# A pre-activation block on one core: where the last centroid rows of two tables are subtracted, and from where the spare rows come

## The chip, the core and the metric

The kernel runs on one core of one Trainium2 chip. The metric is the device time of one execution in microseconds (us). A core has five engines that run side by side, each with its own instruction queue worked off in order: PE (TensorE, matrix products), DVE (VectorE), ACT (ScalarE), POOL (GpSimd) and SP (SyncE, which here only issues DMAs). An engine that waits in front of one instruction holds up all that is queued behind it.

## The reference, cut to what matters

The input x has 32 images of 1024 channels and 14 x 14 positions. Two residual layers are computed. The first one consists of three table layers ("amm"), each followed by a batch norm; the second one is a linear attention and is not touched by the change.

```python
def _amm(patches, centroids, lut, inv_temp):
    v = patches.reshape(B, ncb, sub, H*W).transpose(0, 3, 1, 2)
    scores = 2.0*einsum('blcs,cks->blck', v, centroids) - sum(centroids*centroids, -1)
    attn = softmax(scores*inv_temp, axis=-1)          # over the K = 16 centroids of a codebook
    return einsum('blck,cko->blo', attn, lut)         # lut: codebooks x 16 x outputs

out = _amm(x, c1_centroids, c1_lut, c1_invt)          # layer 1: 256 codebooks of 4 channels, 256 outputs
out = relu(_bn(out, bn1_g, bn1_b))
out = _amm(_extract3x3(out), c2_centroids, c2_lut, c2_invt)   # layer 2: 256 codebooks of 9, 256 outputs
out = relu(_bn(out, bn2_g, bn2_b))
out = _amm(out, c3_centroids, c3_lut, c3_invt)        # layer 3: 64 codebooks of 4, 1024 outputs
return relu(_bn(out, bn3_g, bn3_b) + identity)
```

Layers 1 and 2 have tables of 4096 rows (256 codebooks with 16 rows each) by 256 outputs. Since the 16 weights of a codebook add up to one, a codebook's last row can be subtracted from its other fifteen: that moves the output by a constant per channel, which the batch norm takes out again. The last row's place is then free.

## The kernel before, in words

**Units.** A pass of layers 1 and 2 goes over 16 pairs of images (392 positions) and, in each pair, over 8 units b = 0..7, so over 128 units u = 8 p + b. A unit has four tiles of 128 rows: eight codebooks by 16 centroids. Its steps are: the scores on PE (L897 in layer 1; L1015 and L1024 in layer 2), the exponentials on ACT (L595, written to t), a transpose on DVE (L607), in layer 1 a halving of the sums on POOL (L610), the sum, the reciprocal and a transpose back on DVE (L625, L627, L633), the product with the reciprocals on POOL (L637), and the product with the unit's table on PE (L702, "lut(u)"), which collects all eight units of a pair in two PSUM tiles `po`. ACT's L638 adds up the sums for a check of overflow and waits for the reciprocals. A unit's scores are worked four units (layer 1) or three (layer 2) ahead of its table product; six tiles t rotate.

**Spare rows.** Of four units that follow one another, the first one's first tile (j = 0) is not multiplied as a tile of its own. Its 120 rows other than last ones go into the free last places (rows 15, 31, ...) of the other fifteen tiles, eight rows each. For the weights, POOL writes the tile to `spare` (L635), and small DMAs on SP spread it (L684, `t<-spare`, three or four for each unit). For the tables the same rows have to be in the same places. The eight tables `weights[b]` (512 KB each, named `lut` in the profile) hold a layer's whole table and are loaded again for layer 2.

**Tables before.** For each b, SP issues `own` (L424: the unit's rows), `others` (L427: the spare rows, into every sixteenth partition), and `last_rows`: three or four DMAs that spread each codebook's last row over 16 partitions in a scratch tile d (L439), with a fifth for the spare rows' own last row (L442). One subtraction `v - d` on POOL or DVE (L445, `less`) then ends the table. The scratch lies in the free end of `out1` in layer 1 and in x tiles in layer 2. Layer 1's eight subtractions are put among the first units (`side(i)` runs the pieces that `at(i, ...)` has filed under i, ahead of `lut(i)`); layer 2's eight all stand on POOL after the last unit of layer 1.

**From layer 1 to layer 2.** When lut(127) is done, DVE and POOL work out the norm's scale (L312 to L329, L242), ACT writes the normed images of pair 0 to `pad` (L932, `store_pair`), SP stores them to DRAM (L943, `h1d<-pad`), and SP loads the shifted copies that layer 2's scores need (L963, `patch<-h1d`). Meanwhile DVE builds layer 2's biases and score matrices (L375 on, PE's L390 between), and PE runs dummy products (`warm`, L590). Order on each engine in these layers is the order in which the program issues; nothing reorders it.

**PSUM.** `ps_po` has three rotating buffers; before, only the table products use them. Four more hold scores.

Of the kernel before, what the change touches and what calls it, by code (L numbers as in the profile page):

```python
# [10 lines left out]
F32 = mybir.dt.float32  # L11
AF = mybir.ActivationFunctionType
ALU = mybir.AluOpType
AX = mybir.AxisListType
# [3 lines left out]
P = 128  # L18
C = 1024
CT = C // P  # L20
HW = 196
N2 = 2 * HW
# [3 lines left out]
KC = 16  # L26
W = 256
# [123 lines left out]
def conv_preact_kernel(ctx: ExitStack, tc: tile.TileContext, a: dict, out: bass.AP):  # L151
    nc = tc.nc
    x = a["x"]
    B = x.shape[0]
    NP = B // 2
    NTOK = B * HW
# [37 lines left out]
    ident = const("ident", [P, P], eng=ENG.Activation)  # L194
    mask2 = const("mask2", [72, 8], a["mask2"][1:73])
    bn = {}
    for i, n in ((1, 2), (2, 2), (3, CT)):
        bn[i] = (const(f"bn{i}_g", [P, n]), const(f"bn{i}_b", [P, n]))
    ones = cp.tile([P, P], F32, tag="ones", name="ones")
    nc.vector.memset(ones, 1.0)  # L200
    mhalf = cp.tile([P, 16], F32, tag="mhalf", name="mhalf")
    nc.vector.memset(mhalf, -0.5)
# [209 lines left out]

    def unit_rows(layer, b):
        return lut1_tiles[b] if layer == 1 else lut2_tiles[b // 4, b % 4]

    def packed_lut(layer, b):

        rows, spare = unit_rows(layer, b), unit_rows(layer, b - b % 4)[0]
        j0 = 0 if b % 4 else 1
        k0 = 4 * (b % 4) + j0 - 1  # L420
        v = weights[b].rearrange("p (s w) -> p s w", s=4)

        def own():
            nc.sync.dma_start(v[:, j0:], rows[j0:].rearrange("j c k w -> (c k) j w"))  # L424

        def others():
            nc.sync.dma_start(v[15::16, j0:], spare[:, k0 : k0 + 4 - j0])  # L427

        return v, own, others

    def last_rows(d, layer, b):


        rows, spare = unit_rows(layer, b), unit_rows(layer, b - b % 4)[0]
        j0 = 0 if b % 4 else 1
        v = weights[b].rearrange("p (s w) -> p s w", s=4)
        d = d.rearrange("p (s w) -> p s w", s=4)
        for j in range(j0, 4):
            nc.sync.dma_start(d[:, j], rows[j][:, 15:].to_broadcast([8, KC, W]))  # L439

        def others():
            nc.sync.dma_start(d[15::16, j0:], spare[:, 15:].to_broadcast([8, 4 - j0, W]))  # L442

        def less(engine=nc.gpsimd):
            engine.tensor_tensor(v[:, j0:], v[:, j0:], d[:, j0:], ALU.subtract)  # L445

        return others, less

    sums = cp.tile([P, 3], F32, tag="sums", name="sums")
    sc3 = cp.tile([P, CT], F32, tag="sc3", name="sc3")  # L450
# [75 lines left out]
    def layers(exact, early=None):  # L526
# [59 lines left out]
        def warm(n, rhs):  # L586

            t = scores(rhs.shape[1])
            for _ in range(n):
                nc.tensor.matmul(t, ident, rhs, start=True, stop=True)  # L590
# [70 lines left out]
        def unit_tiles(n):  # L661
# [6 lines left out]
            return ts  # L668


        spares = [
            (dram if exact else big).tile([P, N2], F32, tag=f"spare{exact}{k}", name=f"spare{k}")
            for k in range(2)
# [71 lines left out]
        with ExitStack() as s:  # L745
# [11 lines left out]
            def at(i, piece):  # L757
                todo.setdefault(max(i, -AHEAD - 1), []).append(piece)
# [46 lines left out]
                    at(8 * p + c - AHEAD - 1 - (p == 0), normalise(p, c))  # L805
            at(24, edges)
            at(40, masks2)
            for b in range(8):
                if b > 5:
                    at(b - 6, lambda b=b: load_rows(b))  # L810
                if b > 3:
                    at(b - 5, lambda b=b: others(b))
                engine = nc.vector if b in (3, 5, 7) else nc.gpsimd
                at(b - 3 if b > 1 else -99, lambda b=b, engine=engine: lasts[b][1](engine))

            def later():
                if not exact:
# [3 lines left out]
                load_raw2()  # L821

            at(16, later)

            lasts2, room = {}, {}

            def load_last2(b, k, n):
                def piece():
                    if n == 0:
                        room[k] = xp.tile([P, CT, N2], F32, tag="x", name=f"x_{NP + k}")  # L830
                    d = room[k].rearrange("p c n -> p (c n)")[:, n * C : (n + 1) * C]
                    lasts2[b] = last_rows(d, 2, b)

                return piece

            end = 8 * NP
            for k, bs in ((0, (3, 4, 5)), (1, (0, 1, 2)), (2, (6, 7))):
                for n, b in enumerate(bs):
                    i = end - 8 * (2 - k) + n + (0 if k < 2 else -3)
                    at(i, load_last2(b, k, n))  # L840
                    at(i + 1, lambda b=b: lasts2[b][0]())
            for b in range(7):
                at(end - 7 + b, luts2[b][1])
                if b < 6:
                    at(end - 6 + b, luts2[b][2])

            luts = [packed_lut(1, b) for b in range(8)]

            lasts = []

            def load_rows(b):
                luts[b][1]()
                d = out1[:, b // 4, NTOK - (b % 4 + 1) * C :][:, :C]
                lasts.append(last_rows(d, 1, b))

            def others(b):
                luts[b][2]()
                lasts[b][0]()

            xts[0] = load_x(xp, 0)  # L860
            for b in range(6):
                load_rows(b)
                if b == 1:
                    xts[1] = load_x(xp, 1)
                if b % 2 == 0 and b:
                    others(b - 2)
                    others(b - 1)
            if not exact:
                masks()
            bias1, biases = score_biases(ps_tr, once, st, 1, raw[1], P, CT, mask8, 4)  # L870
            w1 = score_matrices(once, 1, "", raw[1], mask8)
            gn = [
                gn_pieces(sm, ps_tr, xts[p], gn_a[:, :, v], gn_b[:, :, v])
                for p, v in ((0, slice(0, 2)), (1, slice(2, 4)))
            ]
            warm(14, xts[0][:, 0, :HW])
            for f in gn[0][:-1]:
                f()
            if not exact:
                kmasks()  # L880
            ts = unit_tiles(AHEAD + 2)
            biases()
            warm(14, xts[0][:, 1, :HW])
            gn[0][-1]()
            for p in range(2, NP):
                at(8 * p - 17, load(p))
# [25 lines left out]
                halve=not exact,  # L912
            )
            luts2[7][1]()
            luts2[6][2]()
            luts2[7][2]()
            for b in range(8):
                lasts2[b][1]()
            add_up(0, 8 * NP)


        with ExitStack() as s:
# [7 lines left out]
            def store_pair(p, h):  # L930
                t = pads[2 * (p % 2) + h]
                nc.scalar.activation(  # L932
                    t.rearrange("p (i r c) -> p i r c", r=15, c=15)[:, :, :14, :14],
                    out1[:, h, p * N2 : (p + 1) * N2].rearrange(
                        "p (i r c) -> p i r c", r=14, c=14
                    ),
                    AF.Relu,
                    bias=bi1[:, h : h + 1],
                    scale=sc1[:, h : h + 1],
                )  # L940
                for x in range(3):
                    c0 = LEAD + 2 * p * IMG + 1 - DX[x]
                    nc.sync.dma_start(  # L943
                        h1d[16 * h : 16 * h + 16, 8 * x : 8 * x + 8, c0 : c0 + 2 * IMG], t
                    )
# [10 lines left out]
            def load_patches(n, b0=0, m=4, js=range(4)):  # L956
                p, h = divmod(n, 2)
                for j in js:
                    for r0, dy, k in TAPS:
# [7 lines left out]
                            ),  # L967
                        )

            store_pair(0, 0)  # L970
            load_patches(0, 0, 1)
            load_patches(0, 1, 3)
            warm(8, pads[0][:, :N2])
            store_pair(0, 1)
            bias2, biases = score_biases(
                ps_tr,
                once,
# [56 lines left out]

            def side2(i):

                if i == -ahead:
                    for t in pads[2:]:
                        nc.gpsimd.memset(t, 0.0)
                p = {1: 1}.get(i + ahead, (i + ahead + 9) / 8)  # L1040
                if p in range(1, NP):
                    for h in range(2):
                        store_pair(int(p), h)
                if i == 60:
                    bias3, biases = score_biases(ps_tr, big, st, 3, raw[3], P, 2, mask8, 4)
# [906 lines left out]
```

## Time and profile before

| what | value |
|---|---|
| three runs | 3828.63, 3838.37, 3839.19 us; median 3838.37 |
| the profiled execution | 3842.74 us, its span 3840.9 us, mean granted PE clock 0.981 |
| busy share of the span | PE 95%, DVE 78%, POOL 61%, PEld 53%, ACT 44% |
| layer 1, by the trace | first table product at 48.9 us, last one ends at 871.2 us |
| layer 2, by the trace | first scores at 900.2 us, first table product at 919.4 us |
| DMA queue of SP | 260.41 MB, 25.7% of 16 engines |
| L445 (the subtractions) | layer 1: 5 on POOL, 3 on DVE; layer 2: 8 on POOL, median 2337 ns |

PE is named busiest, but a busy share is a mean over stages; what follows is read from two short stretches, the first 110 us and 830 to 960 us, since all that the change touches lies there. PEclk or the clock column of a table by windows is the share of full clock that PE was granted. In a timeline row the columns are start, busy time, engine, line, operation, operands, count, and in brackets the idle time before it with what ended it. A PE row of float32 has two records for one product of the program.

### The profile page before, as it was taken

To read this page: it belongs to the slowest core of one execution; us is meant where nothing else is said; L and a number is where in the kernel's file an instruction comes from. 1 tells how busy PE (TensorE), PEld (TensorE's weight loads), DVE (VectorE), ACT (ScalarE), POOL (GpSimd) and SP (SyncE) were. 2 spreads that over 40 slices of the span, in tenths; PEclk is the share of its full clock that TensorE was granted. 3 is DMA by queue.
4 is the path that set the end of the run, shared out by engine and by line. 5 is a ranking of instruction groups with operands and counts; after the bars stand their busy time and mean duration, and the time that the engine had idled before them with its cause. 6 is when DMAs were issued, how large, how long until landed. Compare 5 with 4: busy or idle time off the path is not lost. (4 is left out here: it accounts for less than half of the span.)

```text
span 3840.9 us, 49292 instructions
## 1 busy us (share of the span) xinstructions
PE 3655.9 (95%) x16211; PEld 2045.9 (53%) x16211; DVE 3008.7 (78%) x4287; ACT 1697.0 (44%) x3851; POOL 2334.6 (61%) x1407
## 2 busy tenths in 40 slices
PE   6899999997999999999999999998999999999998
PEld 4455555543445545454444444444666666666665
DVE  7989999976888888888633333332699999999996
ACT  3455555542333323333212221122766676667764
POOL 6989999984455445544411111111888878878886
PEclk8999999998999999999999999998999999999999
DMA  5111111125444434344211111013123223222221
GB/s 143 44 43 42 37 31 41 42 63 120 92 93 89 94 74 96 77 94 84 58 39 47 39 39 39 20 39 120 48 73 96 79 81 89 84 81 83 83 81 34
DMA packets 243007, 263.78 MB, mean 69 GB/s; under 512 B 32784, under 2 KB 240496, under 8 KB 242744
## 3 DMA queue, kind: packets, MB, share of 16 engines
q1 hardware_dynamic: 242168, 260.41, 25.7%
q8 instruction: 130, 2.13, 0.2%
q14 instruction: 133, 1.09, 0.1%
q10 hardware_dynamic: 576, 0.15, 0.0%
HBM read 171.88 MB, written 76.56 MB: 65 GB/s over the span
## 5 line engine op out<-in xcount | busy, mean ns | idle before, releaser
L637 POOL TENSOR_TENSOR t<-t,r 128x1664 f32<-128x1664 f32 (+2 forms) x284 | 1006.7, 3545 | 1012.7 <-DVE r L633 834.6
L702 PE MATMUL po<-t,lut 128*128 128x392 f32 x3840 | 1343.5, 503 | 29.8 <-DMA t<-spare 25.8
L702 PEld LDWEIGHTS po<-t,lut 128*128 128x128 f32 x3840 | 715.3, 192 | 627.3 <-issue 132.7
L595 ACT ACTIVATE t<-sc,cbias 128x392 f32<-128x392 f32 (+1 forms) x1136 | 578.9, 592 | 946.3 <-issue 473.0
L1462 PE MATMUL mm<-y,lut 128*128 128x392 f32 x2048 | 717.7, 497 | 4.8 <-DVE q L1479 3.2
L1128 PE MATMUL po<-t,lut 128*128 128x448 f32 x1792 | 683.2, 542 | 1.6 <-issue 1.6
L607 DVE STREAM_TRANSPOSE tt<-t 128x1664 f32<-128x1664 f32 (+1 forms) x284 | 542.0, 1909 | 124.4 <-ACT t L595 111.7
L633 DVE STREAM_TRANSPOSE r<-rc 128x1664 f32<-128x1664 f32 (+1 forms) x284 | 546.6, 1925 | 20.5
L1684 DVE SCALAR_TENSOR_TENSOR pa<-y,lepe_w,pa 128x406 f32<-128x406 f32 x900 | 541.9, 639 | 19.2 <-PE pa L1666 16.3
L1128 PEld LDWEIGHTS po<-t,lut 128*128 128x128 f32 x1792 | 339.6, 191 | 342.1 <-issue 341.9
L1462 PEld LDWEIGHTS mm<-y,lut 128*128 128x128 f32 x2048 | 373.7, 190 | 255.5 <-issue 10.7
L1137 DVE BATCH_NORM_STATS2 stats<-o 128x6 f32<-128x448 f32 x112 | 69.0, 617 | 490.0 <-ACT o L1136 490.0
L625 DVE TENSOR_REDUCE sm<-tt 128x104 f32<-128x832 f32 (+2 forms) x284 | 423.3, 1491 | 14.8 <-POOL tt L610 9.4
L610 POOL TENSOR_TENSOR tt<-tt 128x832 f32<-128x832 f32 x128 | 249.4, 1949 | 10.3 <-DVE tt L607 10.3
L1136 ACT COPY o<-po 128x448 f32<-128x448 f32 x112 | 59.0, 527 | 428.1 <-PE po L1128 383.8
L627 DVE RECIPROCAL rc<-sm 128x104 f32<-128x104 f32 (+1 forms) x284 | 229.5, 808 | 9.8
L1015 PE MATMUL sc<-patch,cw 64*128 64x392 f32 x1024 | 210.2, 521 | 7.1 <-DMA patch<-h1d 5.0
L638 ACT ACTIVATE sm<-sm 128x104 f32<-128x104 f32 (+1 forms) x284 | 84.9, 299 | 234.7 <-DVE rc L627 232.8
L1647 POOL TENSOR_TENSOR qr<-qr,zb 128x784 f32<-128x784 f32 x64 | 117.6, 1849 | 68.7 <-DMA zb<-zd 67.1
L1015 PEld LDWEIGHTS sc<-patch,cw 64*128 64x128 f32 x1024 | 90.8, 186 | 116.9 <-issue 67.6
L1471 ACT ACTIVATE e<-mm,kbd 128x392 f32<-128x392 f32 x128 | 74.2, 580 | 168.1 <-PE mm L1462 165.0
L1315 ACT ACTIVATE w<-x,tb,gn_a 128x196 f32<-128x196 f32 x248 | 128.1, 517 | 30.4 <-DVE x L1329 14.0
(183 smaller groups left out, 4108.5 us busy)
## 6 DMA issues: line engine op xcount, KB each, us to landing
patch<-h1d SPq DMA_DIRECT2D x248, 162.8 KB
x<-in_x_dram SPq DMA_DIRECT2D x32, 784.0 KB
o3d<-o SPq DMA_DIRECT2D x14, 1792.0 KB
x<-in_x_dram SPq DMA_DIRECT2D x64, 392.0 KB
out_dram<-x SPq DMA_DIRECT2D x64, 392.0 KB
o<-o3d SPq DMA_DIRECT2D x62, 392.0 KB
h1d<-pad SPq DMA_DIRECT2D x96, 225.0 KB
t<-spare SPq DMA_DIRECT2D x960, 12.2 KB
```

Source lines behind the costliest of these rows:

```text
L595: nc.scalar.activation(t[:, j, : sc.shape[1]], sc, AF.Identity if exact else AF.Exp, bias=bias[:, j : j + 1],)
L607: nc.vector.transpose(tt, tf)
L610: nc.gpsimd.tensor_tensor(tv[:, :, :8], tv[:, :, :8], tv[:, :, 8:], ALU.add)
L625: nc.vector.tensor_reduce(sm, tv, AX.X, ALU.add)
L627: nc.vector.reciprocal(rc, sm)
L633: nc.vector.transpose(r, bc(rc, 2, KC))
L637: nc.gpsimd.tensor_tensor(tf, tf, r, ALU.mult)
L702: nc.tensor.matmul(po[h], luts[b][:, j, h * P : (h + 1) * P], ts[u % len(ts)][:, j, :N2], start=(b == 0 and j == j0), stop=(b == 7 and j = ...
L1015: nc.tensor.matmul(sc, w8[r, 8 * h + 4 * (j // 2) + g], grid(pbuf[n % NPB][r, j // 2, g]), start=True, stop=False,)
L1128: nc.tensor.matmul(po, luts[g][:, m * P : (m + 1) * P], t3[h][:, g % 4, :], start=(g == 0), stop=(g == 7),)
L1462: nc.tensor.matmul(pv(), w[kt][:, m0 : m0 + P], ywin(p, first + kt), start=(kt == 0), stop=(kt == 3),)
L1684: nc.vector.scalar_tensor_tensor(acc, neighbours(p, c, offset(k)), lw[:, c, k : k + 1], acc, ALU.mult, ALU.add,)
```

## The change

The subtraction is done by a product on PE. A matrix `less_last` (128 x 128: the identity, less a one in each codebook's last row in every column of that codebook) is built by three DVE instructions (`last_masks`) from `ident` and `kmask`, which is now worked out ahead of the centroid preparation. A table is loaded whole (`own`: all four tiles, one DMA); `less` multiplies each half of 512 columns by `less_last` into a `po` buffer, and ACT copies it back over the half. The last rows become zero. For the first unit of each four, `keep` writes the first tile so treated to DRAM (`tables`), and `others` reads the spare rows from there. No last rows are loaded, so L439, L442 and L445 are gone.

In layer 1 the loads of tables 0 and 1 stand ahead of the images of pair 1 and the rest right behind; `less` of tables 0 and 1 stands in the preparation, and of 2 to 7 in the iterations i = -4, -3, -2, -2, -1, 0, after that iteration's scores, exponentials and spare rows, ahead of lut(i). In layer 2 the loads stand in the last iterations of layer 1; `less` of tables 0 and 1 stands ahead of the first `store_pair`, that of 2 ahead of and that of 3 behind the second one; `keep(0)` and `others` of 0 to 3 follow on SP; tables 4 to 7 follow in the first four iterations. There are fewer dummy products: 8 and 4 for 14 and 14 at the start, and the 8 after layer 1 are gone. The tile `ones` shrinks to one column.

```diff
-        def own():
-            nc.sync.dma_start(v[:, j0:], rows[j0:].rearrange("j c k w -> (c k) j w"))
-        def others():
-            nc.sync.dma_start(v[15::16, j0:], spare[:, k0 : k0 + 4 - j0])
...
-        for j in range(j0, 4):
-            nc.sync.dma_start(d[:, j], rows[j][:, 15:].to_broadcast([8, KC, W]))
-        def others():
-            nc.sync.dma_start(d[15::16, j0:], spare[:, 15:].to_broadcast([8, 4 - j0, W]))
-        def less(engine=nc.gpsimd):
-            engine.tensor_tensor(v[:, j0:], v[:, j0:], d[:, j0:], ALU.subtract)
...
+        def last_masks():
+            nc.vector.tensor_reduce(cb, ident.rearrange("p (c k) -> p c k", k=KC), AX.X, ALU.add)
+            nc.vector.tensor_scalar(cb, cb, kmask[:, KC - 1 :], None, ALU.mult)
+            v = lambda t: t.rearrange("p (c k) -> p c k", k=KC)
+            nc.vector.tensor_tensor(v(less_last), v(ident), bc(cb, 2, KC), ALU.subtract)
...
+            def own():
+                nc.sync.dma_start(v, unit_rows(layer, b).rearrange("j c k w -> (c k) j w"))
+            def less():
+                for h in range(2):
+                    t = weights[b][:, 512 * h : 512 * h + 512]
+                    ps = ps_po.tile([P, 512], F32, tag="po", name="less")
+                    nc.tensor.matmul(ps, less_last, t, start=True, stop=True)
+                    nc.scalar.copy(t, ps)
+            def keep():
+                nc.sync.dma_start(tables[2 * layer - 2 + b // 4], v[:, 0])
+            def others():
+                nc.sync.dma_start(v[15::16, j0:], kept[:, k0 : k0 + 4 - j0])
...
+            for b, i in ((2, -4), (3, -3), (4, -2), (5, -2), (6, -1), (7, 0)):
+                for k in (2, 3, 4):
+                    if k != 3 or b == 4:
+                        at(i, lambda b=b, k=k: luts[b][k]())
...
-            for b in range(7):
-                at(end - 7 + b, luts2[b][1])
-                if b < 6:
-                    at(end - 6 + b, luts2[b][2])
+            for b in range(7):
+                at(8 * NP - 7 + b, luts2[b][1])
...
             luts2[7][1]()
-            luts2[6][2]()
-            luts2[7][2]()
-            for b in range(8):
-                lasts2[b][1]()
...
+            luts2[0][2]()
+            luts2[1][2]()
             store_pair(0, 0)
             load_patches(0, 0, 1)
             load_patches(0, 1, 3)
-            warm(8, pads[0][:, :N2])
+            luts2[2][2]()
             store_pair(0, 1)
+            luts2[3][2]()
+            luts2[0][3]()
+            for b in range(4):
+                luts2[b][4]()
...
+                for b in range(4, 8):
+                    if i == max(b - 7, -ahead):
+                        luts2[b][2]()
+                        if b == 4:
+                            luts2[b][3]()
+                        luts2[b][4]()
```

`packed_lut` returns the view, `own`, `less`, `keep` and `others`, so that `luts[b][2]` is `less`, `[3]` `keep` and `[4]` `others`; before, it returned the view, `own` and `others`, and `last_rows` returned its own `others` and `less`.

More of the change, by code (lines that the diff above doesn't have):

```diff
@@ L198, in conv_preact_kernel @@
         bn[i] = (const(f"bn{i}_g", [P, n]), const(f"bn{i}_b", [P, n]))
-    ones = cp.tile([P, P], F32, tag="ones", name="ones")
+    ones = cp.tile([P, 1], F32, tag="ones", name="ones")
     nc.vector.memset(ones, 1.0)
@@ L414, in unit_rows @@
         return lut1_tiles[b] if layer == 1 else lut2_tiles[b // 4, b % 4]
[L416 to L421, printed above, removed]
-        def own():
-            nc.sync.dma_start(v[:, j0:], rows[j0:].rearrange("j c k w -> (c k) j w"))
-        def others():
-            nc.sync.dma_start(v[15::16, j0:], spare[:, k0 : k0 + 4 - j0])
[L429 to L437, printed above, removed]
-        for j in range(j0, 4):
-            nc.sync.dma_start(d[:, j], rows[j][:, 15:].to_broadcast([8, KC, W]))
-        def others():
-            nc.sync.dma_start(d[15::16, j0:], spare[:, 15:].to_broadcast([8, 4 - j0, W]))
-        def less(engine=nc.gpsimd):
-            engine.tensor_tensor(v[:, j0:], v[:, j0:], d[:, j0:], ALU.subtract)
-        return others, less
     sums = cp.tile([P, 3], F32, tag="sums", name="sums")
@@ L668, in unit_tiles, with packed_lut @@
             return ts
+        cb = big.tile([P, 8], F32, tag="cblock", name="cblock")
+        less_last = big.tile([P, P], F32, tag="less_last", name="less_last")
+        tables = dram.tile([4, P, W], F32, tag=f"tab{exact}", name="tables")
+        def last_masks():
[3 more added lines that the diff above has]
+            nc.vector.tensor_tensor(v(less_last), v(ident), bc(cb, 2, KC), ALU.subtract)
+        def packed_lut(layer, b):
+            v = weights[b].rearrange("p (s w) -> p s w", s=4)
+            kept = tables[2 * layer - 2 + b // 4].rearrange("(c k) w -> c k w", k=KC)
+            j0 = 0 if b % 4 else 1
+            k0 = 4 * (b % 4) + j0 - 1
+            def own():
[10 more added lines that the diff above has]
+                nc.sync.dma_start(v[15::16, j0:], kept[:, k0 : k0 + 4 - j0])
+            return v, own, less, keep, others
         spares = [
@@ L807, in layers @@
             at(40, masks2)
-            for b in range(8):
[L809 to L814, printed above, removed]
+            for b, i in ((2, -4), (3, -3), (4, -2), (5, -2), (6, -1), (7, 0)):
+                for k in (2, 3, 4):
+                    if k != 3 or b == 4:
+                        at(i, lambda b=b, k=k: luts[b][k]())
             def later():
@@ L823, in layers @@
             at(16, later)
[L825 to L841, printed above, removed]
             for b in range(7):
-                at(end - 7 + b, luts2[b][1])
-                if b < 6:
-                    at(end - 6 + b, luts2[b][2])
+                at(8 * NP - 7 + b, luts2[b][1])
             luts = [packed_lut(1, b) for b in range(8)]
-            lasts = []
-            def load_rows(b):
+            xts[0] = load_x(xp, 0)
+            for b in range(2):
                 luts[b][1]()
[L853 to L867, printed above, removed]
+            xts[1] = load_x(xp, 1)
+            for b in range(2, 8):
+                luts[b][1]()
             if not exact:
                 masks()
+                kmasks()
+            last_masks()
             bias1, biases = score_biases(ps_tr, once, st, 1, raw[1], P, CT, mask8, 4)
@@ L875, in layers @@
             ]
-            warm(14, xts[0][:, 0, :HW])
+            warm(8, xts[0][:, 0, :HW])
+            luts[0][2]()
+            luts[0][3]()
+            luts[0][4]()
             for f in gn[0][:-1]:
                 f()
-            if not exact:
-                kmasks()
             ts = unit_tiles(AHEAD + 2)
             biases()
-            warm(14, xts[0][:, 1, :HW])
+            luts[1][2]()
+            luts[1][4]()
+            warm(4, xts[0][:, 1, :HW])
             gn[0][-1]()
@@ L914, in layers @@
             luts2[7][1]()
-            luts2[6][2]()
-            luts2[7][2]()
-            for b in range(8):
-                lasts2[b][1]()
             add_up(0, 8 * NP)
```

## The prediction

> **What bounds the kernel now.** First the table of busy time by windows: engine columns are busy us (instructions), then granted PE clock, DMA share, GB/s.
>
> ```profile
> 40.00:50.00 10.00, 3.78 (x14) 2.28 (x15) 9.83 (x12) 6.33 (x16) 7.35 (x5) 0.50 0.45 134
> 600.00:650.00 50.00, 49.27 (x196) 25.54 (x192) 49.38 (x58) 27.07 (x66) 48.15 (x21) 1.00 0.14 40
> 850.00:900.00 50.00, 29.61 (x76) 16.03 (x76) 18.13 (x35) 2.40 (x4) 22.49 (x13) 0.76 0.46 133
> ```
>
> In the steady part of layer 1 (600 us) PE and DVE are both full, so work put there costs its whole length. The change puts none there: all of it lies at the start and in the passage to layer 2, where PE has gaps and runs at a reduced clock. So I followed those two in the timeline. The start:
>
> ```profile
> 32.55 4.10 POOL L445 TENSOR_TENSOR lut<-lut,out 128x768 f32<-128x768 f32 x2 [10.36 <-DMA out<-in_lut_dram]
> 36.60 3.79 POOL L610 TENSOR_TENSOR tt<-tt 128x832 f32<-128x832 f32 x2
> 38.56 1.02 DVE L625 TENSOR_REDUCE sm<-tt 128x104 f32<-128x832 f32 x1 [5.59 <-POOL tt L610]
> ...
> 48.88 7.17 PE L702 MATMUL po<-t,lut 128*128 128x392 f32 x12 [3.08 <-POOL tt L610]
> ...
> 73.45 5.50 PE L702 MATMUL po<-t,lut 128*128 128x392 f32 x16 [3.23 <-DMA t<-spare]
> ...
> 82.08 5.88 PE L702 MATMUL po<-t,lut 128*128 128x392 f32 x12 [2.25 <-DMA t<-spare]
> ```
>
> POOL waits for last rows, subtracts, and only then halves the first units' sums; DVE waits for that. Later SP, held by the loads of last rows, brings the spare rows late to lut(3) and lut(4). The passage:
>
> ```profile
> 853.29 17.88 PE L702 MATMUL po<-t,lut 128*128 128x392 f32 x48 [5.28 <-DMA t<-spare]
> ...
> 873.72 17.36 POOL L445 TENSOR_TENSOR lut<-lut,x 128x768 f32<-128x768 f32 x8
> ...
> 875.57 2.28 DVE L328 TENSOR_TENSOR bi<-mv,sc 128x1 f32<-128x1 f32 x1
> ...
> 883.99 1.89 SPq L943 DMA_DIRECT2D h1d<-pad  x3
> 891.10 10.81 SPq L963 DMA_DIRECT2D patch<-h1d  x24
> 891.11 0.57 DVE L375 COPY croom<-mask 72x128 f32<-72x128 f32 x1 [10.77 <-POOL lut L445]
> ...
> 900.19 1.59 PE L1015 MATMUL sc<-patch,cw 64*128 64x392 f32 x8
> ```
>
> Layer 1 ends at 871.17 (853.29 + 17.88; call this E) and layer 2's first scores stand at 900.19: 29.0 us with hardly any useful work. Two chains fill it: SP's last-row loads push the store of `pad` to 883.99, and POOL's eight subtractions hold both the patches and DVE's bias work until 891.1.
>
> **What the Trainium skill says.**
> - "SBUF — State Buffer", section "Who interferes with whom": DVE and GpSimd share a port pair as an exclusive lock; a DVE instruction with two SBUF inputs contends with a GpSimd one that reads. The trace agrees: L328 took 2.28 us beside POOL's subtractions, 0.16 us just before them.
> - "TensorE: Matmul & The Clock Gate", section "What's actually happening": an idle array falls to half clock. The trace agrees: 0.50 at 40 to 50 us. The new products fall where the array may be cold; I price both.
> - "DMA: Bandwidth & Descriptors", section "Anatomy of one DMA": a DMA's fixed cost, about 2 us, is mostly the receipt of the write. Here the last `h1d` store was issued by 885.9 and was landed by about 888.3 (SP's wait for POOL before L963 is 2.8 us, ending at 891.1): 2.4 us, which I use for `keep`.
> - The same page, "Queues, rings and completion order": descriptors are consumed in ring order. So `keep(0)` lands behind the tables issued before it.
>
> **The change part by part.**
>
> *New work.* PE: 8 tables x 2 halves of 128x512 per layer. The L702 record takes 0.344 us at 392 columns (5.5 us / 16), so 0.45 us at 512, twice 0.45 a product: 1.8 us a table warm, 3.6 cold. ACT: the 392-column copy L712 takes 0.48 us; 0.6 at 512, 1.2 us a table, 9.6 per layer.
>
> *Start, to the first scores.* The masks and `kmask` now wait on DVE for `ident`, which lands at 9.9; before, DVE prepared centroids from 2.95. New DVE order: ident 9.9, masks 1.0, preparation 4.4 (3.20 to 3.63 and 7.30 to 11.26), 16 statistics 4.3: 19.6 against 15.5. Before, PE's dummy products hid 1.1 us of that, so the means move by 3.0, and the first scores, then held 1.4 us by dummy products, by 1.7. If `less(1)` ahead of them runs cold, add up to 3. Last rows out of the way bring x of pair 1 and the tables sooner: some 7.4 MB at about 210 GB/s, done by 37 us.
>
> *Start, to lut(0).* t0 is transposed at 29.3 to 32.4 (29.28 before), halved at once, and reciprocals stand at 37.2 to 40.2 instead of 40.4. But `less(7)` is a new wait: lut(0) uses the PSUM buffer that `less(7)` filled, ACT's copy of it stands behind L638 of unit 2, and that behind DVE's reciprocal. Chain on DVE: reciprocals of unit 2 at 49.2 to 52.3, ACT's sum and normalisation 1.5, copy 0.6. So lut(0) starts at 51.3 to 54.4, 2.4 to 5.5 later. `keep(0)` (landed about 38), four `others` and the spare rows (unit 0 at about 45) are ready sooner.
>
> *Start, pair 0.* From lut(0) to the end of lut(7) took 59.0 us (48.88 to 107.86). Gone are the waits 3.23, 2.25 and smaller ones, and DVE's and POOL's subtractions (three of about 2 us on DVE). Left is PE: 7.2 cold, then six units of 6.4 and one of 5.0: 50.5. Saved 8.5, less 2.4 to 5.5: **5 us** gain (3 to 6). The stall at 176 to 188 us, behind SP's constants, stays and moves along.
>
> *Tail of layer 1.* SP keeps `own`, which waits only for the units' own table products, and loses L439, L442 and L427 from the queue ahead of L684. Spare rows of 126 and 127 then leave when POOL ends (849.4, 853.1) instead of 854.1 and 858.6, and PE runs from 843.3 without the waits of 0.49 and 5.28: end 864 to 865.5. **6.5 us** (4 to 7).
>
> *Passage.* Times from E. PE does `less` 0 and 1 by E+3.6; ACT's copies end at E+4.3, `store_pair` at E+5.0 (E+1.3 before), the `h1d` DMAs are issued by E+6.9 and landed at E+9.3. Twelve patch DMAs (0.45 each) and their landing 2.4: scores at E+17.1. DVE's bias chain, free from about E+3.5, with PE's L390 behind `less` 2 and 3 at E+7 to 9 and five dummy products, ends by E+13: hidden, even cold. 29.0 - 17.1: **11.8 us** (8 to 12.5).
>
> *Ramp of layer 2.* On SP, `keep(0)` (0.4), its landing 2.4 and four `others` (2.4) now stand ahead of the next patches, which before waited there for a store anyway: 1.6 late. `keep(4)` with `others` adds the rest ahead of three more patches: 4.1 late, partly under other waits. The spare rows of unit 0 go 1.4 late, the patches that PE awaited at 929.13 about 1.8. `less` 4 to 7 fall into PE's waits. Layer 2 is bound by PE after, so nothing is recovered: **-2.5 us** (-1 to -6).
>
> Smaller `ones`, fewer dummy products: nothing; they ended ahead of the scores or beside a wait, and `less` stands in their place. If that cover goes, the cost is the cold clock, in the ends above.
>
> **Sum:** 5 + 6.5 + 11.8 - 2.5 = 20.8 us less. Against the profiled execution, 3842.7 (span 3840.9): 3821.9. That execution lies 4.4 above the median, 3838.4, so the forecast for the median is **3818**.
>
> **The rivals.**
> - *Only the passage pays* (about 8 to 10 us, 3830). For it: lut(0) starts later, DVE begins later, and PE and ACT have new instructions in order; the start could be worth nothing and layer 2's ramp could cost 6. Against it: the waits on L684 and on POOL are plain rows and their causes leave.
> - *Round trips through memory hold SP* (slower, 3851). Each `keep` must land before `others` may go, and spare rows, stores and patches queue behind. If `keep(0)` waits for tables that come at 134 GB/s (the rate at 40 to 50 us), 7.4 MB need 55 us, and lut(0) starts at about 62: 13 late, less the 8.5 saved. If in layer 2 both trips take 8 us rather than 2.4, that adds 11; two patch sets that PE then awaits add 5 each, and an array left cold 5 more: 30.5 lost against 18.3 of tail and passage, +12. It decides once `keep` to `others` takes more than some 7 us at both places. Against it: 210 GB/s at 10 to 30 us, and 2.4 us for the store.
> - *The loads were hidden anyway*: PE would find another wait in the passage, such as cold scores or the bias chain; then 11.8 shrinks to 5 and the sum to 14. It is inside the first case's range.
>
> **Numbers.** Main case 0.74 (own range 3806 to 3827), only the passage 0.16 (3827 to 3838), round trips 0.10 (to 3855). The range 3804 to 3835 leaves out about a fifth; it holds the low ends (3 + 4 + 8 - 6 = 9) less the 5 us by which equal runs differ, and the high ones (30 with 4 of spread). A change of 0.3%, 11.5 us, is about what a measurement of this kernel can tell from none. Faster by more 0.76, within 0.15, slower by more 0.09.
>
> **What would show it.** Right: no L445; lut(0) later than 48.9 yet lut(7) ended by about 103; no wait for spare rows near 850; from layer 1's end to the first scores of layer 2 some 17 us; the next patches a little late. Wrong: lut(0) after 58, SP waiting on `tables` for more than 5 us, `less` products at cold clock holding the scores, or first scores of layer 2 still 25 us after the end.

## The result and the profile after

The kernel after takes **3808.51 us** (median of 4 runs, 3807.61 to 3810.71). Beside it the kernel before took 3836.49 (4 runs, 3828.63 to 3839.19): a ratio of 0.9931, 95% interval 0.9914 to 0.9948, or 28.0 us less. The forecast was 3818 with a range of 3804 to 3835: right in sign and inside the range, but 9.5 us above the measured time, with 20.8 us of gain for 28.0. The profiled execution of after took 3808.56 (span 3806.8, granted clock 0.988), so it stands on its median; that of before (3842.74) stands 6.2 above the median of before.

First the table of busy time by windows of after, for the same three stretches as before (engine columns busy us and instructions, then PE clock, DMA share, GB/s):

```profile
40.00:50.00 10.00, 6.36 (x30) 2.57 (x22) 9.86 (x8) 7.92 (x20) 9.48 (x4) 1.00 0.08 25
600.00:650.00 50.00, 49.27 (x194) 25.71 (x193) 49.38 (x57) 27.26 (x67) 48.15 (x21) 1.00 0.14 41
850.00:900.00 50.00, 41.17 (x125) 17.09 (x125) 37.73 (x49) 20.32 (x43) 14.97 (x9) 0.86 0.57 145
```

The steady part is unchanged, as it should be. At 40 us PE now runs at clock 1.00 where it had 0.50, with the tables long loaded (25 GB/s against 134); at 850 us PE works 41 of 50 us instead of 30, at 0.86 instead of 0.76 (this window begins at the end of layer 1 in after and 21 us ahead of it in before, so it doesn't hold the same work).

The timeline of after, start of layer 1:

```profile
8.01 5.41 PE L557 MATMUL sc<-x,ident 128*128 128x196 f32 x16 [8.01 <-DMA ident<-in_ident_dram]
...
19.49 1.34 SPq L667 DMA_DIRECT2D tables<-lut  x1
...
27.15 8.08 SPq L670 DMA_DIRECT2D lut<-tables  x4
...
31.16 1.93 POOL L577 TENSOR_TENSOR tt<-tt 128x832 f32<-128x832 f32 x1 [7.85 <-DVE tt L574]
...
34.76 0.98 DVE L592 TENSOR_REDUCE sm<-tt 128x104 f32<-128x832 f32 x1
...
45.59 0.82 PE L706 MATMUL po<-t,lut 128*128 128x392 f32 x2
...
50.16 5.25 PE L706 MATMUL po<-t,lut 128*128 128x392 f32 x10 [3.75 <-ACT lut L664]
...
93.82 5.51 PE L706 MATMUL po<-t,lut 128*128 128x392 f32 x16
```

POOL halves the first sums at once (31.16; before 36.60), and DVE's sum follows at 34.76 (before 38.56). lut(0) starts at 45.59 with two records, stops for the predicted wait on ACT's copy of the last `less` (3.75 us), and ends at 55.41; before it ran from 48.88 to 56.05. From there to lut(7) no wait for spare rows is left, and lut(7) ends at 99.33 instead of 107.86.

And the passage to layer 2:

```profile
825.40 25.29 PE L706 MATMUL po<-t,lut 128*128 128x392 f32 x76
...
850.52 7.03 PE L663 MATMUL less<-lut,less_last 128*128 128x512 f32 x16
...
855.38 1.90 SPq L911 DMA_DIRECT2D h1d<-pad  x3
...
859.68 10.32 SPq L931 DMA_DIRECT2D patch<-h1d  x24
...
862.37 0.90 PE L989 MATMUL sc<-patch,cw 64*128 64x392 f32 x2 [0.67 <-DMA patch<-h1d]
...
867.11 1.69 PE L998 MATMUL sc<-pad,wm 32*128 32x392 f32 x8
...
872.29 0.73 SPq L667 DMA_DIRECT2D tables<-lut  x1
...
876.59 2.46 SPq L670 DMA_DIRECT2D lut<-tables  x4
...
882.87 0.35 SPq L667 DMA_DIRECT2D tables<-lut  x1
...
887.69 0.57 SPq L670 DMA_DIRECT2D lut<-tables  x1
...
889.71 1.85 SPq L688 DMA_DIRECT2D t<-spare  x3
...
893.94 5.80 PE L706 MATMUL po<-t,lut 128*128 128x392 f32 x12 [7.17 <-DMA t<-spare]
```

Layer 1's table products run to E = 850.7 without a wait. The store of `pad` leaves at E + 4.7 (E + 12.8 before), the first scores start at E + 11.7 (E + 29.0) and the first unit's scores end at E + 18.1 (E + 31.5). Then the other side shows: after each `keep` (L667) SP stands still until it has landed, and the first table product of layer 2 waits 7.17 us for spare rows.

**Where the 28 us are.** One trace of each kernel would put the terms at 11.0, 9.6 and 7.3, but starts differ by some 3 us from trace to trace. So I use all traces below that share a stage, old form or new form; a version whose edit lies in a stage is left out of that stage. The marks are the starts of the second of ACT's two copies `out<-po` that close each pair (99.37 in after for pair 0), so a pair is said below to end where that copy starts.

| stage | old form: traces, mean | new form: traces, mean | gain | predicted |
|---|---|---|---|---|
| start, to the end of pair 2 | 219.4 to 222.2, 220.7 (before, e2, e3, e4) | 211.2 to 213.7, 212.9 (after, e1, e5, both e10) | 7.8 | 5 |
| tail, end of pair 13 to E | 100.1 to 101.7, 100.9 (before, e1, e3, e9) | 92.0 to 92.4, 92.1 (after, e2, e4 to e8, both e10) | 8.8 | 6.5 |
| passage and ramp, E to the end of layer 2's pair 0 | 110.5 to 114.1, 112.2 (before, e1, e9) | 105.2 to 106.8, 105.8 (after, e2, e6, e7, both e10) | 6.4 | 11.8 - 2.5 = 9.3 |
| layer 4, last copy of layer 3 to the end | 1183.1 to 1184.3, 1183.7 (before, e1, e3, e9) | 1176.9 to 1180.8, 1178.5 (after, e2, e5, e7, e8, e10_after_planA) | 5.2 | 0 |

They add up to 28.2, against 28.0 by the medians. The first three, which the change touches, give 23.0 where the prediction had 20.8.

### The profile page after: what moved, and what is told of

Same layout as the page of the kernel before. It is cut to its first block, busy times and chain, and to the rows that moved or that the text cites. A ratio compares the mean times of both kernels' runs of the same rounds, so it can differ in the third digit from the quotient of the medians.

```text
span 3806.8 us, 49254 instructions
## 1 busy us (share of the span) xinstructions
PE 3657.1 (96%) x16227; PEld 2040.3 (54%) x16227; DVE 2998.0 (79%) x4287; ACT 1711.6 (45%) x3883; POOL 2304.0 (61%) x1394
## 5 line engine op out<-in xcount | busy, mean ns | idle before, releaser
L600 DVE STREAM_TRANSPOSE r<-rc 128x1664 f32<-128x1664 f32 (+1 forms) x284 | 546.5, 1924 | 20.8 <-DVE rc L594 0.5
L989 PEld LDWEIGHTS sc<-patch,cw 64*128 64x128 f32 x1024 | 88.8, 185 | 114.1 <-issue 62.0
```

What stands on the lines that cost most here:

```text
L600: nc.vector.transpose(r, bc(rc, 2, KC))
L989: nc.tensor.matmul(sc, w8[r, 8 * h + 4 * (j // 2) + g], grid(pbuf[n % NPB][r, j // 2, g]), start=True, stop=False,)
```

## Experiments

e1 to e4 ran beside a before of 3836.79 us (31 runs), e5 to e8 beside one of 3837.12 (7 runs), e9 to e11 beside one of 3837.42 (19 runs). The edits of e3, e4 and e9 are shown against before, all others against after.

**e1_new_layer1 and e2_new_layer2: each half of the change alone.** e1 keeps layer 2's loads and subtractions as in before, e2 those of layer 1; e2 builds `less_last` in the steady part.

```diff
 # e1: layer 2 keeps the old form
-            luts2 = [packed_lut(2, b) for b in range(8)]
+            luts2 = [old_lut(2, b) for b in range(8)]
...
 # e2: layer 1 keeps the old form
+            at(41, last_masks)
...
-            luts = [packed_lut(1, b) for b in range(8)]
+            luts = [old_lut(1, b) for b in range(8)]
...
```

> The kernel before with the change in layer 1 alone; layer 2's tables keep their loads of last rows and the subtractions on POOL. In the trace of the changed kernel the gain stands at 8.5 us when the first pair ends, 10.9 in the steady part of layer 1, 20.5 at its end and 27.8 after the first pair of layer 2. Theory (the three places are independent): only the first 10.9 us come, 3836.5 - 10.9 = 3825.6; the waits of PE for spare rows before the end of layer 1 (1.74 + 0.49 + 5.28 us) and the 29 us of passage are back as before. Rival (a lead won at the start is what takes away the waits at the end of layer 1): the 20.5 us come, 3816. Rival (the start is worth only what the first pair shows, the rest is noise of one trace): 3828.

> The kernel before with the change in layer 2 alone (layer 1 prepares its tables as before; the difference matrix is built in iteration 41). Theory (independent places): 9.6 us at the end of layer 1 and 7.3 in passage and first pair of layer 2: 3836.5 - 16.9 = 3819.6. Rival (the end of layer 1 gains only with the lead from the start): about 7 to 9 us, 3829. With the run of the change in layer 1 alone the two savings should add up to 28 us if the parts are independent, and to clearly less or more if not.

Measured: e1 3825.59 us (10 runs), ratio 0.9973 (0.9964 to 0.9983), 11.2 less; e2 3820.80 (6 runs), 0.9961 (0.9949 to 0.9974), 16.0 less. Together 27.2 of 28.0: the halves are independent as far as these runs tell, and both pay. Layer 2's half had been put at 6.5 + 11.8 - 2.5 = 15.8, layer 1's at 5. From pair 2 to pair 13 e2 took 551.3 us and after 547.4. The trace shows where, in `last_masks` in the full part: its second instruction, on 128 x 8 numbers, took 0.23 us in after, with POOL idle, and here

```profile
330.11 3.71 POOL L637 TENSOR_TENSOR t<-t,r 128x1664 f32<-128x1664 f32 x1 [1.34 <-ACT x L813]
330.18 3.66 DVE L677 TENSOR_SCALAR cblock<-cblock,kmask 128x8 f32<-128x8 f32 x1
```

It ended with POOL's product. That pair of images took 55.3 us instead of 50.4.

**e9_no_sub1_A: what made the start slow.** Before, with layer 1's eight subtractions left out (the tables are used undiminished) and their loads kept; the order of engines in layer 4's planner is fixed as in e10 below.

```diff
-                at(b - 3 if b > 1 else -99, lambda b=b, engine=engine: lasts[b][1](engine))
...
-        engines = {p[0] for p in self.pieces}
+        engines = ["PE", "DVE", "ACT", "POOL", "SP"]
```

> The kernel before with layer 1's eight subtractions of last rows left out (lut's rows are used without the difference), their loads kept, layer 4's order fixed as in before. Theory (the start's 10.9 us came mainly from POOL's and DVE's subtractions ahead of the sums and of lut 0): layer 1's pair 0 ends at about 100 us instead of 107.9 and the kernel takes 3829 us (8 less). Rival (it came mainly from SP's loads of last rows, which stay, with the waits of 3.23 and 2.25 us for spare rows): pair 0 ends at 103 to 105 us and the kernel takes 3833 us.

Measured: 3827.64 us (16 runs), ratio 0.9973 (0.9965 to 0.998), 9.8 less. Pair 0 ends at 98.98 and pair 2 at 210.76, as early as in after (99.37 and 211.22). Its timeline has no wait for spare rows among the first table products. PE's rows:

```profile
48.55 6.47 PE L702 MATMUL po<-t,lut 128*128 128x392 f32 x12 [8.45 <-issue]
...
55.82 5.53 PE L702 MATMUL po<-t,lut 128*128 128x392 f32 x16
...
62.16 5.53 PE L702 MATMUL po<-t,lut 128*128 128x392 f32 x16
...
68.49 5.53 PE L702 MATMUL po<-t,lut 128*128 128x392 f32 x16
...
74.83 4.22 PE L702 MATMUL po<-t,lut 128*128 128x392 f32 x12
```

SP's own rows of that stretch, in the same timeline:

```profile
58.23 2.56 SPq L439 DMA_DIRECT2D out<-in_lut_dram  x4
...
60.91 3.11 SPq L684 DMA_DIRECT2D t<-spare  x4
...
66.90 2.54 SPq L439 DMA_DIRECT2D out<-in_lut_dram  x4
...
69.55 2.33 SPq L684 DMA_DIRECT2D t<-spare  x3
```

Every load of last rows (L439) is still there, ahead of spare rows (L684). So leaving out the subtractions on POOL and DVE is enough for all that the change gains at the start, and the loads issued ahead of each group of spare rows cost PE nothing once the subtractions are gone. The way is seen in unit 3, whose spare rows lut(3) awaited at 73.45. In before POOL ended its weights at 66.86:

```profile
63.13 3.73 POOL L637 TENSOR_TENSOR t<-t,r 128x1664 f32<-128x1664 f32 x1
66.04 2.56 SPq L439 DMA_DIRECT2D out<-in_lut_dram  x4
68.72 3.11 SPq L684 DMA_DIRECT2D t<-spare  x4
```

and in e9 at 57.83:

```profile
54.12 3.71 POOL L637 TENSOR_TENSOR t<-t,r 128x1664 f32<-128x1664 f32 x1
```

Of what SP waited for in before between 45 and 90 us, 12.6 us were POOL's weights.

**e3_no_sub2 and e4_no_load2: what made the passage slow.** e3 is before without layer 2's eight subtractions, their loads kept. e4 keeps the subtractions and leaves out layer 2's loads of last rows; one ACT copy fills each scratch tile instead, so wrong rows are subtracted.

```diff
 # e3
-            for b in range(8):
-                lasts2[b][1]()
...
 # e4
...
+            if layer == 2:
+                nc.scalar.copy(d, out1[:, 0, :C].rearrange("p (s w) -> p s w", s=4))
-            for j in range(j0, 4):
+            for j in range(j0, 4) if layer == 1 else ():
```

> The kernel before, with the eight subtractions of layer 2 left out and all its loads of last rows kept (the output of layer 2 is then not the reference's). It asks which of the two chains held the passage. Theory (SP's queue holds it nearly as long as POOL): the store of the normed images still leaves some 13 us after the end of layer 1, its landing 2.4 us later releases the patches, which before waited another 2.8 us for POOL: 3 us gain, 3833.5, and the waits for spare rows before the end of layer 1 stay. Rival (POOL alone holds it): 13 us, 3823, with the store leaving some 5 us after the end of layer 1.

> The kernel before, with the eight subtractions of layer 2 kept on POOL but its loads of last rows left out: the scratch tile is filled by one ACT copy of other data instead, so that POOL still reads it (the output of layer 2 is not the reference's). Theory: SP's queue was the cause of the waits for spare rows before the end of layer 1, so that end comes 9 to 10 us sooner; the passage stays near 29 us, since POOL's 17.4 us still start 2.5 us after the end of layer 1 and release patches and bias work: 3827. Rival (the waits before the end come from the tables' own loads or from POOL): no gain before the end, 3836. Rival (POOL was no bound in the passage): the passage falls to some 20 us as well, 3818.

Measured: e3 3832.47 us (20 runs), ratio 0.9985 (0.9978 to 0.9992), 4.3 less; e4 3814.41 (4 runs), 0.9945 (0.9928 to 0.9962), 22.4 less, of which about half is another plan of layer 4 (e10). Three rows of the timeline of e3:

```profile
850.11 17.45 PE L702 MATMUL po<-t,lut 128*128 128x392 f32 x48 [4.02 <-DMA t<-spare]
...
880.54 1.90 SPq L941 DMA_DIRECT2D h1d<-pad  x3
...
887.56 0.89 PE L1013 MATMUL sc<-patch,cw 64*128 64x392 f32 x2 [2.23 <-DMA patch<-h1d]
```

and three of e4's:

```profile
861.67 17.37 POOL L744 TENSOR_TENSOR lut<-lut,x 128x768 f32<-128x768 f32 x8
...
879.06 10.32 SPq L966 DMA_DIRECT2D patch<-h1d  x24
...
888.98 1.59 PE L1018 MATMUL sc<-patch,cw 64*128 64x392 f32 x8
```

Without the subtractions (E = 867.56) the tail's wait for spare rows stays, the store of `pad` still leaves at E + 13.0 and the first scores start at E + 20.0: there SP's queue sets them. Most of that is not issue time: between 830 and 892 us in before, SP waits 10.3 us for last rows to land before L442 may write among them, and 5.3 us for L424's rows before L427. Without the loads (E = 859.12) the tail is as short as in after (92.0 us from pair 13), but POOL's 17.37 us hold the patches and the scores start at E + 29.9. The tail is the loads' doing alone; the passage needs both gone.

**e5_early_keep: what `keep` costs the ramp.** After, with the first tiles of layer 2's tables 0 and 4 loaded, multiplied and kept in iterations 60 to 64 of layer 1, so that no `others` waits for a `keep` at the passage.

```diff
+            for k in range(3):       # load, less, keep of the two first tiles
+                at(60 + 2 * k, first_tiles(k))
...
-            luts2[0][3]()
...
```

> The changed kernel, with the two first tiles of layer 2's tables treated and written to memory in iterations 60 to 64 of layer 1 (one product of 512 columns, one copy, four small DMAs), so that no write of spare rows to memory stands in the passage. In the changed kernel SP waits 3.6 and 4.5 us between keep and others there, and PE waits 7.2 us for spare rows before its first table product of layer 2. Theory (the round trips hold SP): first table product of layer 2 some 35 to 38 us after the end of layer 1 instead of 43, but the patches awaited after it limit the gain by the end of the pair: 3 to 6 us, 3803 to 3805.5. Rival (stores and patches hold SP anyway): the waits are filled by the next DMA's own wait, within 1 us, 3808. Cost in layer 1: about 1 us.

Measured: 3805.43 us, ratio to before 0.9918 (0.9901 to 0.9934), 3.1 less than after by the medians, which the intervals do not separate. The timeline says more:

```profile
875.68 2.46 SPq L670 DMA_DIRECT2D lut<-tables  x4
...
891.32 0.90 PE L706 MATMUL po<-t,lut 128*128 128x392 f32 x2 [1.71 <-DMA t<-spare]
...
893.33 3.56 PE L706 MATMUL po<-t,lut 128*128 128x392 f32 x10 [1.11 <-ACT lut L664]
```

E is 853.84 here, so lut(0) of layer 2 starts at E + 37.5 (after: E + 43.3), and pair 0 ends at E + 103.4 (after and its like: 105.8). From pair 2 to E it needs 1.5 more than e6 and both e10 (640.8 against 639.1 to 639.4), probably the price of three pieces put where DVE and PE are full.

**e6_less_sooner: does `less` of the last tables hold layer 1's start?** After, with `less` of tables 4, 6 and 7 one iteration sooner.

```diff
-            for b, i in ((2, -4), (3, -3), (4, -2), (5, -2), (6, -1), (7, 0)):
+            for b, i in ((2, -4), (3, -3), (4, -3), (5, -2), (6, -2), (7, -1)):
```

> The changed kernel, with the difference products of tables 4, 6 and 7 one iteration sooner in layer 1, so that ACT's copy of table 7 no longer stands ahead of the first table product (3.75 us wait of PE, my one new wait). Theory (the gain of the start is set by the chain over DVE, POOL and SP, which reaches the stall at 178 us as early as before): lut(0) about 3 us sooner, but nothing left of it after the stall, 3808.5. Rival (PE's chain sets it): 3 to 4 us are kept, 3805. Rival (ACT's queue gets too full before the first exponentials): 2 us slower.

Measured: 3797.05 us, 0.9892 (0.9875 to 0.9908). The wait on ACT is gone and lut(0) ends at 52.6 instead of 55.4, but then PE waits 2.67 us for spare rows at 62.60. Pair 0 ends at 99.53, pair 2 at 212.77 and layer 2's pair 0 at 957.59 (after: 99.37, 211.22 and 957.45), so nothing of it lasted; the 11.5 us come in layer 4, which the edit does not touch. That led to e10.

**e7_spread and e8_all: the stall behind SP's constants.** In after PE waits once, in pair 2:

```profile
177.78 8.48 PE L706 MATMUL po<-t,lut 128*128 128x392 f32 x16 [10.95 <-DMA t<-spare]
```

because SP issues 29 loads of constants in a block ahead of spare rows. e7 issues them two an iteration; e8 is e5, e6 and e7 together.

```diff
...
-            at(16, later)
+            later()
+            for n, (dst, src) in enumerate(pieces):
+                at(16 + n // 2, lambda dst=dst, src=src: nc.sync.dma_start(dst, src))
```

> The changed kernel, with the 29 loads of constants that stand on SP in iteration 16 spread two to an iteration over iterations 16 to 30. In both kernels PE waits 11 us there for spare rows, and then runs its next products at reduced clock (8.5 us for 5.5). Theory: the stall goes whole and with it 3 us of cold clock, 11 to 14 us: 3796. Since the change was found to keep the gain of DVE's and POOL's chain through this stall, a second question is whether the lead that PE has there of 2 us less is then lost: if PE's chain binds once the stall is gone, the gain falls to 9, 3799.5. Rival (DVE and POOL use the stall to catch up, and are the bound): 3 to 5 us, 3805.

> The changed kernel with the three edits together: spare rows of layer 2 written early, difference products sooner, constants spread. If their gains are independent and as each theory says (4 + 0 + 12, and 2 more from the sooner start once the stall no longer levels it): 3791. If each falls to its rival: 3804.

Measured: e7 3796.90 us, 0.9894 (0.9877 to 0.991); pair 2 ends at 200.08 instead of 211.22 and the row above is gone. e8 3790.66, 0.9878 (0.9861 to 0.9894). In e8 pair 0 of layer 2 ends at E + 101.3.

**e10 and e11: the plan of layer 4.** Layer 4's order is written by a planner that asks the engines in the order of a Python set of strings, which differs from one build of the same source to the next. Fixed lists in its place:

```diff
-        engines = {p[0] for p in self.pieces}
+        engines = ["PE", "DVE", "ACT", "POOL", "SP"]     # e10_after_planA
+        engines = ["POOL", "DVE", "PE", "ACT", "SP"]     # e10_after_planB, e11_all_planB
```

> The kernel after, with the order in which layer 4's planner asks the engines fixed (PE ahead of POOL) instead of left to a set's order. Theory (the planner's tie between engines, decided anew by each build, sets layer 4's order, and after drew the order with PE first): the same as after, 3808.5 us, layer 4 takes 1177.9 us from layer 3's last copy. Rival (differences between builds come from elsewhere): anything from 3797 to 3809.

> The kernel after, with POOL ahead of PE in the planner's list. Theory: layers 1 to 3 as in after (layer 2's pair 0 ends at 957.4 us); layer 4 takes 1169 to 1171 us as in e4_no_load2 and e6_less_sooner, so 3798 us (7 to 11 less than after, 3797.5 to 3801.5). Rival: those two kernels gained their 9 to 11 us by what they changed, and this one stays at 3808.5.

> e8_all (first tiles of layer 2 kept early, less of tables 4, 6 and 7 one iteration sooner, constants spread) with POOL ahead of PE in layer 4's planner. Theory (the gains are in separate stages and add): 3790.7 less 9 to 11, so 3780 to 3782 us. Rival (layer 4's plan is worth what it is only after a late start, or was not the cause): 3788 to 3791.

Measured: plan A 3810.02 us (0.9929, 0.9906 to 0.9951), plan B 3799.05 (0.9902, 0.988 to 0.9925), e8 with plan B 3780.60 (0.9852, 0.983 to 0.9875). The plans are told apart by DVE's order. After has `kmm` ahead of `kv`:

```profile
2687.60 2.45 DVE L1574 TENSOR_TENSOR kmm<-ks,hmean 128x32 f32<-128x32 f32 x2
...
2706.84 0.69 DVE L1550 TENSOR_TENSOR kv<-mm,bmask 128x512 f32<-128x512 f32 x1 [0.70 <-PE mm L1541]
```

e10_after_planB has it behind:

```profile
2705.61 0.69 DVE L1550 TENSOR_TENSOR kv<-mm,bmask 128x512 f32<-128x512 f32 x1 [0.37 <-PE mm L1541]
...
2718.86 1.92 DVE L1574 TENSOR_TENSOR kmm<-ks,hmean 128x32 f32<-128x32 f32 x2
```

From layer 3's last copy to the end, plan A took 1176.9 to 1184.3 us in ten traces and plan B 1168.0 to 1170.6 in four (e4, e6, e10_after_planB, e11_all_planB). The traces of before and after both show plan A, so their difference is not the draw. With plan A, 11.0 us more, e6 would be at 3808 (after: 3808.5) and e4 at 3825 (11 less than before; its marks show 13.2 in the touched part). e11 is the fastest version tried, 57 us under before, about 10 of them from the draw.

## Why the prediction was right or wrong

**Sign and bound: right.** The steady part kept its rows, and PE's gaps at the two ends paid.

**Start: mis-sized, 7.8 by the means (10.0 in e9, 11.0 by the two single traces) for 5.** The saving from lut(0) to lut(7) was predicted well: the rest of pair 0's table products fell from 51.8 us (56.05 to 107.86) to 43.9 (55.41 to 99.33), 7.9 against 8.5. The failed step is what was taken off it, "lut(0) starts at 51.3 to 54.4, 2.4 to 5.5 later". The new wait came exactly where it was named, on ACT's copy of `less(7)`, but it ended at 50.16, lut(0) had done two of its twelve records before it, and although the granted clock was only 0.72 from 50 to 56 us, lut(0) ended 0.6 sooner than before. The two inputs that were too late: `ident` landed by 8.0, not 9.9, and the reciprocal of unit 2 ended at 48.28 (47.48 + 0.80), not at 49.2 to 52.3. The tables came sooner, too: `keep(0)` had landed by 27.15, not 38, as the DMAs moved 341 GB/s from 10 to 20 us and 349 from 20 to 25, where the sum took 210.

**Start, cause: half wrong.** The prediction said "SP, held by the loads of last rows, brings the spare rows late". e9 keeps these loads and loses the waits: the subtractions on POOL and DVE were behind them, and the weights came late. Scratch tiles are not the way, since each of the eight tables has its own area in layer 1 and no load waits for a subtraction there. The loads' own part is at most the 1.9 us from unit 3's weights (66.86) to the issue of its spare rows (68.72); unit 4's left at 78.47, right behind its weights (78.44). A queue that issues something just ahead of a late DMA need not be what made it late.

**Tail: mechanism right, 8.8 for 6.5.** e4 shows that the loads do it and e3 that the subtractions have no part in it. The sum began at 843 us and left out a wait for spare rows of 1.74 us at 801.13, which went too. PE ended at 850.7 by after's own trace, 20.5 sooner than before, of which 11 are the start's.

**Passage: mechanism right, 13.4 for 11.8.** The `h1d` store was landed at E + 9.0, where E + 9.3 was forecast. But the first scores start at E + 11.7 and not at E + 17.1, so what compares is the end of the first unit's scores: E + 18.1 instead of E + 31.5. They do not wait for the twelfth patch, as the sum assumed, but follow the patches one by one, with waits of 0.26 to 0.67 us. Both chains named were needed: e3 leaves SP's at E + 20.0, e4 leaves POOL's at E + 29.9.

**Ramp: just outside its range, -7 for -2.5.** 6.4 for passage and ramp, less 13.4, leaves -7 (-6 by the two single traces). The mis-sized term is the landing of `keep`: SP waited 3.6 us after the first (873.02 to 876.59) and 4.5 after the second (883.22 to 887.69), and 3.9 and 4.3 in e7, where 2.4 had been taken from the `h1d` store. The Trainium skill's "DMA: Bandwidth & Descriptors", section "Anatomy of one DMA", puts the fixed cost at about 2 us, for DMAs issued from GpSimd; here a 128 KB store issued from SP, behind other traffic, took about twice that. e5 takes these waits away and gets back 2.4 us by the stage means (3.4 by single traces), so the rest of the 7 lies elsewhere, perhaps in the other DMAs that share SP with the patches; that was not tried alone.

**Layer 4: not in the prediction, 5.2 us.** Layer 4's instructions follow the same plan in both, yet the traces with the old form of layer 2's tables take 1183.1 to 1184.3 us and those with the new form 1176.9 to 1180.8 (e2: 1180.4). I know no cause. The granted clock doesn't show one (0.93 to 0.95 in its first 100 us in either kind).

**Rivals.** *Only the passage pays* is out: e1 alone gains 11.2 us. *Round trips hold SP* has its mechanism in the ramp, but the trips there stayed under the 7 us from which it was to decide. In layer 1 SP did wait 6.3 us (20.83 to 27.15, or 7.7 from the start of `keep`), more than the 5 us that were named as a sign of being wrong, but nobody waited for SP. *Hidden anyway* holds for e4's passage alone, as long as the subtractions stand.

**The sum: near in part by luck.** 20.8 predicted, 23.0 measured in the touched stages, since errors of +2.8, +2.3 and -2.9 partly cancel. Each of the four terms, 7.8, 8.8, 13.4 and -7, lies outside the range given for it. About 7 us more of the miss are 5.2 in layer 4 and 1.9 from before, whose median moved from 3838.4 to 3836.5. That the result lies inside the range is luck as well: its lower end rests on a gain of 30, but the high ends of the terms add up to 24.5 (6 + 7 + 12.5 - 1). With that and the same 4 of spread it would have stood near 3810, above the 3808.5 measured.

## What to carry to other kernels

Where two chains end at the same place, price each without the other before hoping for the sum: at the first scores of this passage, taking out the loads alone gave nothing and the subtractions alone 9 us, while the change, which takes out both, gave 17. A store to memory that is read back at once is a wait on its queue for all behind it, so put it well ahead of the rush. And before comparing two builds whose order a planner decides, fix every tie in it: an unordered set was worth 11 us here, beside 28 for the change.

## What was not expected of the hardware

A table product with a 128-wide difference matrix and 512 columns is cheap at full clock: the four records of one table in layer 2's ramp took 1.98 us, ACT's copy of one half 0.58 us, both near the estimates of 1.8 and 0.6. The table before it, from 868.73 on, took 3.78 us, with a granted clock of 0.65 from 865 to 870 us; 3.6 had been the estimate.

The clock at the start went with the work: where these products run among the first units, it was 1.00 from 30 to 50 us (after, e6), where they don't, 0.50 to 0.55 (before, e9). In after it fell to 0.72 from 50 to 56 us, behind the 3.75 us in which PE waited for ACT; in e6, without that wait, it stayed at 1.00. By itself the higher clock was worth nothing here: e9, at 0.50, ends pair 2 as early as after.

A small instruction can cost as much as a large one beside it: 128 x 8 numbers on DVE took 3.66 us while POOL's product ran (e2), and 0.23 us with POOL idle.
